# Branch hints on two long jumps, and three own-row gathers ahead of the branches, in a graph-attention and expert-mixture kernel

## The chip, the cores and the metric

The kernel runs on one core of a Trainium2 chip. The time is the device time of one execution in microseconds; the median of the runs is compared. The core has a matrix engine (PE, with its weight loads listed as PEld), a vector engine (DVE), an activation engine (ACT), a general engine (POOL) and a queue engine (SP). Each of them runs its own instruction stream, and all branch for themselves: a condition in the program is a register load and a compare-and-branch on every engine. They wait for each other through semaphores. An instruction that the engine's queue handles alone (a branch, a register load, a semaphore wait) is listed in the profile with a q behind the engine's name and is not counted as busy.

## The reference

1250 nodes with 512 features, 21,250 directed edges sorted by destination. A normalised graph-attention layer is added to `x`; its result is normalised again and goes into a mixture of four experts, each a two-layer SAGE convolution. Each node takes its two best experts.

```python
h = relu(layernorm(x));  x = x + attention(h, edges)
h = relu(layernorm(x))
gates = softmax(h @ gate_W + gate_b);  top_v, top_i = top_k(gates, 2)
for e in range(4):
    z = h
    for l in range(2):
        mean = segment_sum(z[src], dst) * inv_deg
        z = relu(mean @ Wl[e, l] + bl[e, l] + z @ Wr[e, l])
    expert[e] = z
out = x + sum(expert[top_i[n, k]][n] * top_v[n, k] for k in (0, 1))
```

## The kernel before, in words

`tile_sorted_graph` does everything for a graph whose edges are sorted; `tile_any_graph` is a second kernel behind it, which runs only if a count of the edges (`total`) does not come out as expected. Here it comes out, so the last branch, L1404, jumps over all of `tile_any_graph`.

The attention layer and the first aggregation take the first 220 us or so. Then the nodes that chose an expert are numbered (`number_slots`): per expert, its nodes fill places of 128 slots. `many[:, 0]` holds the number of nodes of each expert, `many[:, 1]` whether the number of places is odd; both are loaded into registers of all five engines where they are compared (`loaded`, L762).

The loop over experts starts at L1016. Layer 1 of an expert is computed for all 1250 nodes in five steps (`layer1`); its result goes to DRAM (`h1`) by SP and stays on chip in split form (`hs`). One step of the next expert's layer 1 is put behind the last one, to fill gaps. Layer 2 is computed only for the slots of the expert, place by place:

- The counts of edges of a place's nodes are gathered from DRAM by POOL (`fetch_counts`, L802), transposed and unpacked into a matrix (`unpack`); PE multiplies it with `hs` (`sums_of`, L935), which gives the neighbours' sums.
- The place's own rows of `h1` are gathered by POOL (`fetch_own`, L821) into a tile of the ring `hsels`, which has two tiles, and PE transposes them (`features`, L829).
- If the number of places is odd, `one_of_slots` does the first one alone, under the branch at L1041. The others are done two at a time by `pair_of_slots`, in five bodies nested in each other under the branches at L1043: where `counts[e] > i * 128` fails, the engine jumps over all the bodies that are left.
- A place's result is scattered into the output with addition, by POOL (`put`, L947).

Before the branch at L1041, two places' own rows are gathered (L1029). The third is gathered inside the first pair's body, as its first operation (L1048), and later pairs gather two places for the next pair after the transposes of their own. A new gather into a ring tile waits until the tile's last content has landed and been read.

Every engine runs its instructions in the order in which they were put; POOL's order of gathers, scatters and branches is therefore the order of the code. At the end of each expert POOL drains (L1067).

Of the kernel before, what the change touches and what calls it, by code (L numbers as in the profile page):

```python
# [9 lines left out]
F32 = mybir.dt.float32  # L10
# [3 lines left out]
I32 = mybir.dt.int32  # L14
U32 = mybir.dt.uint32
AF = mybir.ActivationFunctionType
OP = mybir.AluOpType
AX = mybir.AxisListType

SLOPE = 0.2  # L20
EPS = 1e-5
# [21 lines left out]
def tile_sorted_graph(  # L43
# [27 lines left out]
    nc = tc.nc  # L71
    N, D = x.shape
    E = src.shape[0]
    NE = gate_W.shape[1]
    T = 125
    NT = N // T
# [20 lines left out]
    const = ctx.enter_context(tc.tile_pool(name="const", bufs=1))  # L97
# [37 lines left out]
    SLOTS = 128  # L135
    NS = -(-N // SLOTS) + 1
# [15 lines left out]
    nc.gpsimd.memset(many_edges, float(1 << 15))  # L152
    ones_h = const.tile([128, 128], BF16, name="ones_h")
    nc.vector.memset(ones_h, 1.0)
    many = const.tile([1, 2, NE], I32, name="many")
    AT = adj.tile([T, NT, N], F32R, name="AT")
    AT32 = AT.bitcast(F32)

# [114 lines left out]
    for name in ("dst", "src"):  # L273
# [5 lines left out]
        i = build.tile([EB, NB], F32, name=f"i_{name}")  # L279
# [7 lines left out]
    for k in range(KF):  # L287
        for half in range(2):
# [3 lines left out]
                                           op0=OP.mult, op1=OP.mult,  # L292
# [14 lines left out]
    for half in range(2):  # L307
# [3 lines left out]
                                       op0=OP.mult, op1=OP.mult, accum_out=bw_b[:, half, HD:])  # L311
# [352 lines left out]
    def number_slots():  # L664

        flat = chosen.rearrange("p e t -> p (e t)")
        p = bank("p_n")
        nc.tensor.matmul(p[:T, :NE * NT], before, flat, start=True, stop=True)  # L670
        nc.tensor.matmul(p[:T, NE * NT:2 * NE * NT], ones_h[:T, :T], flat, start=True, stop=True)
        pv = p[:T, :2 * NE * NT].rearrange("p (a e t) -> p a e t", a=2, e=NE)
        off = book.tile([T, NE, NT + 1], F32, name="off")
        nc.vector.memset(off[:, :, 0], 0.0)
        for t in range(NT):
            nc.vector.tensor_add(off[:, :, t + 1], off[:, :, t], pv[:, 1, :, t])
        nc.vector.tensor_copy(many[:, 0, :], off[:1, :, NT])

        odd = book.tile([T, NE], F32, name="odd")
        twos = book.tile([T, NE], F32, name="twos")  # L680
        nc.vector.tensor_scalar(odd, off[:, :, NT], 1.0 / SLOTS, 0.5 - 0.25 / SLOTS, op0=OP.mult,
                                op1=OP.add)
        nc.vector.tensor_scalar(odd, odd, ROUND, -ROUND, op0=OP.add, op1=OP.add)
        nc.vector.tensor_scalar(twos, odd, 0.5, -0.25, op0=OP.mult, op1=OP.add)
        nc.vector.tensor_scalar(twos, twos, ROUND, -ROUND, op0=OP.add, op1=OP.add)
        nc.vector.scalar_tensor_tensor(odd, twos, -2.0, odd, op0=OP.mult, op1=OP.add)
        nc.vector.tensor_copy(many[:, 1, :], odd[:1, :])
        at = book.tile([T, NE, NT], F32, name="at")
        nc.vector.tensor_add(at, pv[:, 0], off[:, :, :NT])
        at = at.rearrange("p e t -> p (e t)")  # L690
        qt = book.tile([T, NE * NT], F32, name="qt")
        nc.vector.tensor_scalar(qt, at, 1.0 / SLOTS, -(0.5 - 0.25 / SLOTS), op0=OP.mult, op1=OP.add)
        nc.vector.tensor_scalar(qt, qt, ROUND, -ROUND, op0=OP.add, op1=OP.add)
        nc.vector.scalar_tensor_tensor(at, qt, float(-SLOTS), at, op0=OP.mult, op1=OP.add)

        by_expert = qt.rearrange("p (e t) -> p e t", e=NE)
        nc.vector.tensor_tensor(by_expert, by_expert, odd[:, :, None].to_broadcast([T, NE, NT]),
                                op=OP.subtract)
        nc.vector.scalar_tensor_tensor(qt, qt, 2.0, flat, op0=OP.add, op1=OP.mult)
        left = book.tile([T, NE, NT], F32, name="left")  # L700
        nc.vector.tensor_copy(left, g.rearrange("p t e -> p e t"))
        left = left.rearrange("p e t -> p (e t)")
        for f in range(2, FLD):
            nc.vector.tensor_copy(told[:, :, f], left)
            if f + 1 < FLD:
                nc.vector.tensor_sub(left, left, told[:, :, f])
        for e in range(NE):
            c = slice(e * NT, (e + 1) * NT)
            nc.vector.tensor_tensor(spots[:, c, :], steps_h[:, None, :].to_broadcast([T, NT, SLOTS]),
                                    at[:, c, None].to_broadcast([T, NT, SLOTS]), op=OP.is_equal)  # L710

        mine = mix_tiles[0][0].rearrange("p k n -> p (k n)").bitcast(BF16)[:T, :NE * NT * NS].rearrange(
            "p (c q) -> p c q", q=NS)
        nc.vector.tensor_tensor(mine, steps_h[:, None, 1:NS + 1].to_broadcast([T, NE * NT, NS]),
                                qt[:, :, None].to_broadcast([T, NE * NT, NS]), op=OP.is_equal)
        nc.vector.tensor_tensor(tells, mine[:, :, None, :].to_broadcast([T, NE * NT, FLD, NS]),
                                told[:, :, :, None].to_broadcast([T, NE * NT, FLD, NS]), op=OP.mult)
# [41 lines left out]
    nc.tensor.matmul(p[:T, :1], ones[:T, :T], sums[:, :1], start=True, stop=True)  # L759
    nc.vector.tensor_copy(total, p[:1, :1])  # L760

    def loaded(v, most):  # L762
        return nc.values_load(v, min_val=0, max_val=most,
                              skip_runtime_bounds_check_because="it is compared, and addresses nothing")

    counts, odds = ([loaded(many[:1, i, e:e + 1], N) for e in range(NE)] for i in range(2))
# [23 lines left out]
    packeds = Ring(1, [T, SLOTS], I32, "packed")  # L790
    digs = Ring(2, [T, 2, SLOTS], I32, "digs")
    ASs = Ring(2, [T, NT, SLOTS], F32R, "AS")
    hsels = Ring(2, [SLOTS, D], F32, "hsel")
    rTs = Ring(2, [128, KF, SLOTS], F32, "rT")
    gTs = Ring(2, [128, KF, SLOTS], F32, "gT")
    aggs = Ring(1, [SLOTS, D], F32, "agg")
# [22 lines left out]
    def fetch_own(j, h1):  # L819
        r = hsels()  # L820
        nc.gpsimd.indirect_dma_start(r, None, h1, bass.IndirectOffsetOnAxis(reads[:, j:j + 1], 0))  # L821
        return r
# [193 lines left out]
    for e in range(NE):  # L1016
        now.loads()
        for t in range(min(e, 1), NT // 2):
            now.layer1(t)
            if e == 0 and t == NT // 2 - 2:  # L1020
                asel = [fetch_counts(e * NS + i) for i in range(4)]
            if t == NT // 2 - (1 if e == 0 else 2):
                AS = [unpack(asel.pop(0)) for _ in range(2)]
                if e + 1 == NE:
                    third = wts[(e + 1) % 2].tile([128, KF, D], F32R, name="wl0")
                    third = third.rearrange("p k n -> p (k n)")[:T, :NT * SLOTS]
                    AS.append(unpack(asel.pop(0), third.rearrange("p (s n) -> p s n", s=NT)))
        now.finish()
        own = [fetch_own(e * NS + i, now.h1) for i in range(2)]  # L1029
        of = now  # L1030
        if e + 1 < NE:
            now = Expert(e + 1)
            now.layer1(0)
        mixing = of.mix_second()
        second = next(mixing)
        of.spare_sums = node_sums[4:] + \
            [vs.tiles[(vs.n + i) % 4] for i in range(2)]
        hs, h1 = of.hs, of.h1
        A, iv = AS.pop(0)
        r = own.pop(0)  # L1040
        with tc.If(odds[e] > 0):  # L1041
            one_of_slots(second, r, sums_of(A, hs), iv, e, 0)
        with ExitStack() as nest:  # L1043
            for i in range(1, NS, 2):
                nest.enter_context(tc.If(counts[e] > i * SLOTS))
                j = e * NS + i
                if i == 1:
                    own.append(fetch_own(j + 1, h1))  # L1048
                    if len(AS) < 2:
                        AS.append(unpack(asel.pop(0)))  # L1050
                    second = next(mixing)
                    asel.append(fetch_counts(j + 3))
                p = [sums_of(a, hs) for a, _ in AS]
                ivs = [iv for _, iv in AS]
                g = [mean_of(p[0], ivs[0])]
                r = [features(v, rTs, AF.Relu) for v in own]
                if i + 2 < NS:
                    own = [fetch_own(j + 2 + n, h1) for n in range(2)]
                    AS = [unpack(asel.pop(0)) for _ in range(2)]
                g.append(mean_of(p[1], ivs[1]))  # L1060

                asel += [fetch_counts(j + n) for n in range(4, 6) if i + n < NS]
                pair_of_slots(second, r, g, of.spare_sums, e, i)
        if e + 1 < NE:
            asel = [fetch_counts((e + 1) * NS + i) for i in range(4)]

        tc.keep_in_program_order(nc.gpsimd.drain())  # L1067
# [329 lines left out]
@with_exitstack  # L1397
def tile_gat_then_moe_sage(ctx: ExitStack, tc: tile.TileContext, *args):
    nc = tc.nc
    flag = ctx.enter_context(tc.tile_pool(name="flag", bufs=1))  # L1400
    total = flag.tile([1, 1], I32, name="total")
    counted = tile_sorted_graph(tc, *args, total)
    E = args[1].shape[0]
    with tc.If(counted != E):  # L1404
        tile_any_graph(tc, *args)


# [26 lines left out]
```

## Time and profile before

| what | value |
|---|---|
| median of 3 runs | 770.07 us (769.75 to 770.88) |
| the profiled execution | 766.87 us |
| its span, first to last instruction | 765.1 us |
| mean granted clock of PE | 0.985 |
| places of slots that ran (scatters of L947) | 22 |
| own gathers (L821) / gathers of counts (L802) | 31 / 35 |
| L1043 branches of each engine | 17 |
| transfers of code: queue q8, queue q14 | 35 packets of 0.57 MB, 36 of 0.29 MB |

The profile is one execution. A line of a timeline gives the start in us from the span's start, the busy time, the engine, the line of the code, the operation, the tiles (written <- read) and how often it stands there; in square brackets is how long the engine had stood idle before it, and what released it. A line of waits gives the engine and its operation, behind the arrow what it waited for, and then the total in us, how often, and the longest. A line of queue instructions gives how many, their shortest, median and longest duration in ns, and the starts of the first and the last in us. A window's line gives, for PE, PEld, DVE, ACT and POOL, the busy time and in brackets the number of instructions, then PE's granted clock (1.00 is full), the DMA engines' busy share and GB/s.

### The profile page before, as it was taken

The numbers are of one execution on the slowest core, as the hardware profiler recorded it, in microseconds if no ns is written. First come the engines' busy times: TensorE is split into PE (matmuls) and PEld (weight loads), VectorE is DVE, ScalarE is ACT, GpSimd is POOL, SyncE is SP. The second block draws the span as 40 slices with busy tenths as digits, with TensorE's granted clock in tenths as the row PEclk, the third lists the DMA queues.
The fourth block names the chain that finished last, engine by engine and source line by source line (L and its number), as shares of the span: only waits on it lengthen the run. The fifth ranks groups of instructions, "written<-read, shape, count | busy, mean of one in ns | idle before, by whom it ended". The sixth has DMA issues, their size and how long they took to land. (4 is left out here: it accounts for less than half of the span.)

```text
span 765.1 us, 9962 instructions
## 1 busy us (share of the span) xinstructions
PE 718.2 (94%) x3413; PEld 581.3 (76%) x3413; DVE 515.3 (67%) x1345; ACT 247.6 (32%) x569; POOL 160.4 (21%) x140
## 2 busy tenths in 40 slices
PE   6799989898999999889999999999999999999893
PEld 4677444445999888778878888888888888888782
DVE  7987999799888559336965544568464554657542
ACT  4559656865300112110313332103031333104320
POOL 1001425222002001120033332300142331400441
PEclk9899999999999999989999999999999999999997
DMA  7000001010135412181223133631132322601332
GB/s 199 5 7 5 3 7 58 8 41 1 48 131 175 127 41 70 29 280 39 68 76 58 43 56 56 193 126 41 43 80 44 59 46 45 181 28 56 79 62 31
DMA packets 30147, 52.46 MB, mean 69 GB/s; under 512 B 7132, under 2 KB 8326, under 8 KB 30076
## 3 DMA queue, kind: packets, MB, share of 16 engines
q0 software_dynamic: 6768, 15.51, 11.0%
q1 hardware_dynamic: 15154, 20.18, 8.8%
q10 hardware_dynamic: 8154, 15.91, 6.0%
q8 instruction: 35, 0.57, 0.3%
q14 instruction: 36, 0.29, 0.1%
HBM read 33.03 MB, written 19.20 MB: 68 GB/s over the span
## 5 line engine op out<-in xcount | busy, mean ns | idle before, releaser
L429 PE MATMUL p_o<-hW,P 125*125 125x512 f32 x200 | 91.8, 599 | 3.8 <-DVE P L423 3.7
L935 PE MATMUL p_s<-h_hi,AS 125*128 125x512 f32 x210 | 83.9, 399 | 0.9 <-DVE v L907 0.9
L115 ACT ACTIVATE h_hi<-v 125x512 fp32r<-125x512 f32 x40 | 24.9, 629 | 181.4 <-DVE v L904 144.7
L935 PE MATMUL p_s<-h_lo,AS 125*128 125x512 f32 x210 | 82.0, 390 | 0.0
L839 PE MATMUL p<-T,S 128*125 128x256 f32 x320 | 73.4, 381 | 0.4 <-DVE v L888 0.2
L839 PEld LDWEIGHTS p<-T,S 128*125 128x125 f32 x320 | 60.2, 189 | 10.6 <-DVE v L888 1.6
L941 DVE TENSOR_SCALAR agg<-p_s,asel 128x512 f32<-128x512 f32 x22 | 16.5, 750 | 76.4 <-PE p_f L829 39.4
L816 ACT CAST AS<-digs 125x256 fp32r<-125x256 int32 x150 | 54.8, 403 | 36.9 <-DVE digs L340 31.2
L821 POOL DMA_INDIRECT hsel<-h,reads x31 | 36.1, 1164 | 141.9 <-issue 51.0
L429 PEld LDWEIGHTS p_o<-hW,P 125*125 125x125 f32 x200 | 35.3, 188 | 39.4 <-issue 32.6
L947 POOL DMA_INDIRECT out_dram<-y,writes x22 | 35.8, 1626 | 118.1 <-ACT y L983 47.8
L427 POOL TENSOR_TENSOR den<-den,P 125x375 f32<-125x375 f32 (+1 forms) x27 | 39.3, 1454 | 57.9 <-DVE P L423 51.8
L340 DVE TENSOR_SCALAR digs<-packed 125x128 int32<-125x128 int32 x279 | 45.7, 221 | 3.0 <-ACT packed L810 2.2
L802 POOL DMA_INDIRECT asel<-packs,reads x35 | 38.4, 1097 | 39.3 <-DVE agg L941 25.1
L935 PEld LDWEIGHTS p_s<-h_hi,AS 125*128 125x128 f32 x210 | 39.5, 188 | 9.4 <-issue 1.3
L831 ACT ACTIVATE gT<-p_f 128x512 f32<-128x512 f32 x22 | 13.6, 616 | 99.9 <-PE p_f L829 99.9
L935 PEld LDWEIGHTS p_s<-h_lo,AS 125*128 125x128 f32 x210 | 39.5, 188 | 8.1
L839 PE MATMUL p<-wr,h2T 128*125 128x256 f32 x160 | 39.9, 394 | 6.0 <-DVEq L1043 4.9
L327 PE MATMUL p_h<-W_sb,hT 128*125 128x257 f32 x160 | 40.7, 412 | 3.1 <-ACT hT L184 3.0
L554 PE MATMUL p_ag<-AT,h_hi 125*128 125x416 f32 (+1 forms) x120 | 42.4, 355 | 0.0
L554 PE MATMUL p_ag<-AT,h_lo 125*128 125x416 f32 (+1 forms) x120 | 42.1, 353 | 0.0
L381 DVE TENSOR_SCALAR first<-iota,low,val 125x125 bf16<-125x125 f16 x128 | 40.8, 384 | 0.0
(238 smaller groups left out, 1461.3 us busy)
## 6 DMA issues: line engine op xcount, KB each, us to landing
h<-v SPq DMA_DIRECT2D x40, 224.0 KB
wl<-in_L_gnn_Wl_dram ACTq DMA_DIRECT2D x7, 1024.0 KB
wr<-in_L_gnn_Wr_dram ACTq DMA_DIRECT2D x7, 1024.0 KB
out_dram<-x SPq DMA_DIRECT2D x10, 224.0 KB
x<-in_x_dram SPq DMA_DIRECT2D x1, 1120.0 KB
h<-v SPq DMA_DIRECT2D x40, 26.0 KB
W_sb<-in_L_gnn_W_dram SPq DMA_DIRECT2D x4, 256.0 KB
wl<-in_L_gnn_Wl_dram SPq DMA_DIRECT2D x1, 1024.0 KB
```

The source lines that it names most:

```text
L327: nc.tensor.matmul(p[:T, :HD + 1], hT[:, k, :], W_sb[:, k, half, :], start=(k == 0), stop=(k == KF - 1))
L340: nc.vector.tensor_scalar(o, v, BITS * d, (1 << BITS) - 1, op0=OP.logical_shift_right, op1=OP.bitwise_and)
L381: nc.vector.tensor_scalar(hs[:, :T], iota[:EB, :T], low[:, j:j + 1], val[:, j:j + 1], op0=OP.is_equal, op1=OP.mult)
L427: nc.gpsimd.tensor_add(den[:, :n], den[:, :n], P[:, :n])
L429: nc.tensor.matmul(po[i][:T, :], P[:, i * T:(i + 1) * T], hW[:, s - 1, :, :HD], start=(s == 1), stop=(s == NT))
L554: nc.tensor.matmul(p[:, :n], h2[s][i][:, m * 128:(m + 1) * 128], AT[:, s, c], start=(s == 0 and i == 0), stop=(s == NT - 1 and i == 1))
L802: nc.gpsimd.indirect_dma_start(a, None, packs, bass.IndirectOffsetOnAxis(reads[:, j:j + 1], 0))
L816: nc.scalar.copy(AS[:, d:d + 2, :], dig)
L821: nc.gpsimd.indirect_dma_start(r, None, h1, bass.IndirectOffsetOnAxis(reads[:, j:j + 1], 0))
L839: nc.tensor.matmul(p, A[:, k, :], B[:, k, :], start=(i == 0 and k == 0), stop=(i * KF + k == n - 1))
L935: nc.tensor.matmul(p, A[:, s, :], hs[s][f], start=(s == order[0] and f == 0), stop=(s == order[-1] and f == 1))
L947: s = nc.gpsimd.indirect_dma_start(out, bass.IndirectOffsetOnAxis(writes[:, j:j + 1], 0), y, None, bounds_check=N - 1, oob_is_err=False, c ...
```

## The change

Three things are edited.

1. The two kinds of jump get a name (`label`), and a hint instruction is put ahead of the branch. For the first pairs branch of expert 0 (`pairs0`) it stands ahead of the branch at L1041, on DVE and POOL only, and takes its value from a register: a new row of `many`, 1 if the expert has more than 128 nodes (the body runs) and 0 if not (the jump is taken). For the branch around `tile_any_graph` (`general`) it stands in the first pair body of the last expert, on PE, DVE, ACT and POOL, with no register: the jump is expected to be taken.
2. The third gather of own rows moves from the first pair's body to the two others, ahead of both branches of the expert, in every expert.
3. The ring `hsels` gets a third tile.

`loaded` now names the engines; its default is the same five as before.

```diff
+ET = mybir.EngineType
+HINTED = [ET.PE, ET.DVE, ET.Activation, ET.Pool]
...
-    many = const.tile([1, 2, NE], I32, name="many")
+    many = const.tile([1, 3, NE], I32, name="many")
...
         nc.vector.tensor_copy(many[:, 1, :], odd[:1, :])
+        nc.vector.tensor_scalar(many[:, 2, :], off[:1, :, NT], SLOTS + 0.5, None, op0=OP.is_gt)
...
-    def loaded(v, most):
-        return nc.values_load(v, min_val=0, max_val=most,
+    def loaded(v, most, engines=(*HINTED, ET.SP)):
+        return nc.values_load(v, engines=engines, min_val=0, max_val=most,
...
-    hsels = Ring(2, [SLOTS, D], F32, "hsel")
+    hsels = Ring(3, [SLOTS, D], F32, "hsel")
...
-        own = [fetch_own(e * NS + i, now.h1) for i in range(2)]
+        own = [fetch_own(e * NS + i, now.h1) for i in range(3)]
...
         hs, h1 = of.hs, of.h1
+        if e == 0:
+            some = (ET.DVE, ET.Pool)
+            tc.mark_branch_hint_location("pairs0", hint=loaded(many[:1, 2, :1], 1, some), engines=some)
         A, iv = AS.pop(0)
         r = own.pop(0)
         with tc.If(odds[e] > 0):
             one_of_slots(second, r, sums_of(A, hs), iv, e, 0)
         with ExitStack() as nest:
             for i in range(1, NS, 2):
-                nest.enter_context(tc.If(counts[e] > i * SLOTS))
                 j = e * NS + i
+                nest.enter_context(tc.If(counts[e] > i * SLOTS, label="pairs0" if j == 1 else None))
+                if e + 1 == NE and i == 1:
+                    tc.mark_branch_hint_location("general", engines=HINTED)
                 if i == 1:
-                    own.append(fetch_own(j + 1, h1))
                     if len(AS) < 2:
                         AS.append(unpack(asel.pop(0)))
...
-    with tc.If(counted != E):
+    with tc.If(counted != E, label="general"):
         tile_any_graph(tc, *args)
```

## The prediction

> **What bounds the kernel now.** I read the page's engine table first, then who waited for whom on PE, then the one gap that this list names in PE's own timeline, then the tail behind the last transfer.
>
> ```profile
> span 765.1 us, 9962 instructions
> PE 718.2 (94%) x3413; PEld 581.3 (76%) x3413; DVE 515.3 (67%) x1345; ACT 247.6 (32%) x569; POOL 160.4 (21%) x140
> ```
>
> PE is busy 94% of the span. From 200 to 300 us the list of waits has no entry for PE, so work added there on DVE (busier than PE in places) costs nothing. From 300 us on, PE waited for this (releaser; us in total, times, longest):
>
> ```profile
> PE p L839 <- DVEq L1043: 4.9, 1, 4.9
> PE p_f L829 <- DMA hsel<-h,reads: 2.4, 1, 2.4
> PE p L839 <- DVE y L991: 1.1, 2, 0.5
> PE p_s L935 <- DVE v L907: 0.9, 1, 0.9
> ```
>
> Two gaps matter. The first is released by DVE's queue at L1043, the nested branch, and not by an operation. PE's timeline around it, and DVE's queue there (start of first and last):
>
> ```profile
> 321.62 1.89 PE L839 MATMUL p<-T,agT 128*125 128x256 f32 x8
> 328.45 3.75 PE L839 MATMUL p<-wr,h2T 128*125 128x256 f32 x8 [4.95 <-DVEq L1043]
> ```
> ```profile
> L1043 DVEq COMPARE_BRANCH  x1: 69/69/69, 324.0 to 324.0; - x1
> L1043 DVEq EVENT_SEMAPHORE  x1: 21/21/21, 328.3 to 328.3; - x1
> ```
>
> Expert 0 has one place of slots (the L947 rows are 1, 8, 9 and 4 for the four experts), so its first nested branch jumps over five pair bodies. DVE branches at 324.0 for 0.07 and runs its next instruction at 328.3: 4.2 us of nothing, in which the trace has an 8 KB transfer of the instruction queue q14 (326.4). PE's own branch shows the same as a long duration, with a 16 KB transfer of q8 inside it (322.2, 1.1 us):
>
> ```profile
> L1043 PEldq COMPARE_BRANCH  x1: 3512/3512/3512, 321.2 to 321.2; - x1
> L1043 PEldq EVENT_SEMAPHORE  x1: 51/51/51, 324.8 to 324.8; - x1
> ```
>
> So PE is ready at 324.8 and stands until 328.45 for DVE alone. The gap costs more than itself. Windows by stage (after the sums and engine columns: granted clock, DMA share, GB/s):
>
> ```profile
> 323.00:328.00 5.00, 0.51 (x3) 0.10 (x1) 0.42 (x1) 0.00 (x0) 0.18 (x1) 0.77 0.54 126
> 328.00:330.00 2.00, 1.54 (x4) 1.29 (x5) 0.00 (x0) 0.00 (x0) 0.89 (x1) 0.50 0.42 42
> ```
>
> The clock went to 0.50 at 325.7 and back to 1.00 at 332.5; the eight matmuls at 328.45 took 3.75 us, where eight of that shape take 1.89 before.
>
> The second gap is in expert 3, whose first pair has nothing of a next expert beside it:
>
> ```profile
> 712.90 0.94 POOL L821 DMA_INDIRECT hsel<-h,reads  x1 [2.28 <-PE p_f L829]
> 716.31 0.66 PE L829 MATMUL p_f<-ident,hsel 128*128 128x128 f32 x4 [2.45 <-DMA hsel<-h,reads]
> ```
>
> The gather issued last holds PE for 2.45. Last, the tail: POOL's last scatter starts at 754.0 and lands at 759.1; then POOL's queue reaches the branch around the general kernel, L1404, and again jumps:
>
> ```profile
> L1404 POOLq COMPARE_BRANCH  x1: 55/55/55, 760.2 to 760.2; - x1
> L1404 POOLq EVENT_SEMAPHORE  x1: 17/17/17, 762.8 to 762.8; - x1
> ```
>
> 2.5 us stand between them. PE passes L1404 at 758.1, DVE at 758.4, SP at 706.0; so POOL alone sets the end of 765.1.
>
> **The change part by part.**
>
> *Hint on the first pairs branch, DVE and POOL.* No row of before shows a hint, so bounds first. At worst it does nothing; at best DVE resumes as after its other taken branches, 0.05 to 0.5 us behind them (L1043 at 485.5: 0.3). Then DVE is through at 324.0 + 0.07 + 0.3 = 324.4. What is late next is PE's own jump, which gets no hint here: 324.8, plus its semaphore and first weights, 0.15 as at 328.3 to 328.45, so 325.0. Saved: 328.45 - 325.0 = 3.45. PE then stands 1.5 us. The gap of 2.45 in expert 3 kept a clock of 1.00, so I expect no slow stretch: the first ten matmuls after 328.45 spread over 4.2 us where 0.216 each makes 2.15, saved 2.05. Together 5.5. Behind it PE has no wait over 0.6 until 702, and the weight loads that ACT issues after waiting for DVE (328.4) move ahead with it, so the gain is kept. I take the full value, because the hint stands 17 us ahead of the branch (DVE's previous branch is at 306.5) and the fetch itself took under 4.3. Its price: one register load on DVE (L763 DVEq rows, 0.30 to 0.91), inside the 4.42 us that DVE stands before L941 at 311.25; on POOL (0.28 to 0.51) inside 16 us idle before 321.1. If that cover were gone, at most 1 us. POOL needs no such hint: it went on 0.13 after its branch at 321.4. The new comparison in number_slots is one 4-element DVE operation (L681: 0.15) at about 220, where PE waits for nothing.
>
> *Third gather ahead of the branches, ring of three.* In expert 3 the gathers start at 707.64, 709.68 and 712.90. The third waits until 712.2, when the first has landed, because with two tiles it overwrites that one; it also stands behind two branches of POOL. With three tiles it follows the second after 0.94 and the usual 0.30, at 710.9, and lands 3.41 later as before (712.90 to 716.31): 714.3. PE is free at 713.87, so it waits 0.5 in place of 2.45: 2.0 saved, and behind it every row of expert 3 shifts. Queued behind the moved gather on POOL are the register load, the scatter of an odd place and the gathers of counts; in expert 2 it moves from 560.2 to about 542.7 with POOL idle until 558.1, in expert 1 from 389.7 to 387.9, and PE waits for none of these. Expert 0 gets one gather more (about 305.3, 0.94 us, its rows unread), with POOL idle behind it. The free third tile also ends much of POOL's 41.0 us of waiting for p_f; PE does not wait for those, so nothing.
>
> *Hint on the general branch, four engines.* It is put into expert 3's first pair body, four instructions; no row has their cost, nearest are POOL's register moves and branches, 0.03 to 0.07, on PE inside its 0.95 wait at 702. PE, DVE and ACT are off the path at the end. For POOL the 2.5 goes to between 0.13 (its taken L1043 at 753.8, next instruction at 754.0) and 0.38 (SP at L1404); I take 0.2: 2.3 saved. Late next are SP's waits, done at 760.4, the same instant, then POOL's drain of 1.36 and the closing handshake as now.
>
> Sum: 5.5 + 2.0 + 2.3 = 9.8. The profiled execution took 766.87 around its span of 765.1; it would become 757.1. The median of the runs is 770.07, 3.2 above it; I take the same difference off the median: **760.3**.
>
> **A rule against the change.** The trace shows that each long jump ends with a transfer on an instruction queue. The Trainium skill (Runtime: NRT & Kernel Launch, Instruction fetch mechanics) says that prefetch of code is purely sequential, and that a taken branch to a page outside the current two forces a fetch before execution goes on; it knows no hint. By it both hints do nothing and the change is worth 2.0. The trace of before agrees with its second half (4.2, 3.5 and 2.5 us) and cannot show the first.
>
> **The rivals.**
>
> 1. *Hints do not act* (0.13). Only the gather's 2.0 is left: 768.1. For it: no row shows a hint acting. Against it: a branch 17 us away leaves time.
>
> 2. *The first hint comes too late, the last one acts* (0.15). The q14 transfers near DVE are at 294.3, 321.7 and 326.4, and DVE has 64 recorded rows from 294 to its branch. If the one at 294.3 already filled DVE's next block, a hint at 306 finds the slot taken. Then 2.0 + 2.3 are left: 765.8.
>
> 3. *The first acts, POOL's last does not* (0.08), since POOL lands only 6 us ahead of L1404: 5.5 + 2.0, so 762.6.
>
> 4. *Slower* (0.12). A hint takes the slot of the next block at once and holds it until its branch. The last hint is armed at about 705, and four engines then run 45 us of straight code. PE fetches at 729.9 and 749.9 in this stretch, DVE crosses about one border. DVE's would cost what L1043 costs today, 4.95 + 2.05 = 7.0; PE's two each 3.5 less the 2.3 that its queue ran ahead at 321.2, up to 5.6 without that lead and with the slow clock: 9.4 to 18.2 against 9.8 saved, so -0.4 to +8.4, in the middle +4: 774. It decides once PE's two crossings cost over 1.4 each. Against it: PE's queue passes its branch at 725.7 while the matmuls ahead of it run until 729.7, a lead of 4.
>
> **How the numbers follow.** The forecast has 0.52. Cases to 768.1 hold 0.88 with it; the low end adds 1.8 below 760.3 for a jump of PE that shortens too (its 1.5 left) and rounding, the high end is rival 1 and 0.5: 758.5 to 768.6. A measurement tells about 0.2%, 1.5 us, from no change: forecast and rivals 2 and 3 are faster (0.75), rival 1 at 2.0 is mostly so (0.08, and 0.05 within), rival 4 is slower (0.12).
>
> **What would show it.** Right: DVE's first instruction behind its L1043 within 0.5 us; PE's gap there about 1.5, with a clock of 1.00 until the end; a q14 transfer between 306 and 323; expert 3's three gathers 1.2 apart, PE's wait there under 0.7; POOL's L1404 pair under 0.4 apart. Wrong: DVE still 4 us late at L1043 (rivals 1, 2); new long branch or idle "issue" rows on PE and DVE in expert 3 (rival 4); a clock of 0.50 after a gap of 1.5.

## The result and the profile after

The changed kernel takes **760.29 us** (median of 4 runs, 759.65 to 761.53); the kernel before, timed beside it, takes 770.48 (769.75 to 772.25). The ratio is 0.9866 with an interval of 0.9845 to 0.9888. In a later comparison (`after_again`, below) it was 762.07 against 769.58, ratio 0.9893 [0.9864, 0.9922]. So the change gains 1.1 to 1.3%, and the forecast of 760.3 holds. Its terms do not all hold, and that is what the rest is about.

The profiled execution of the changed kernel took 760.18 us. Line numbers have moved: the nested branch is L1049 (was L1043), the last branch L1411 (L1404), the own gathers L824 (L821), the scatter L950 (L947). First the page's first lines, then what PE waited for from 300 us on:

```profile
span 758.5 us, 9991 instructions
PE 717.9 (95%) x3413; PEld 580.6 (77%) x3413; DVE 516.4 (68%) x1346; ACT 247.7 (33%) x569; POOL 158.9 (21%) x141
```
```profile
PE p L842 <- DVEq L1049: 2.3, 1, 2.3
...
PE p_f L832 <- DMA hsel<-h,reads: 0.4, 1, 0.4
```

PE's work is the same; its two named waits went from 4.9 to 2.3 and from 2.4 to 0.4. PE's timeline around the first one, the queue instructions there, and the window with PE's granted clock:

```profile
323.87 1.89 PE L842 MATMUL p<-T,agT 128*125 128x256 f32 x8
328.05 1.96 PE L842 MATMUL p<-wr,h2T 128*125 128x256 f32 x8 [2.29 <-DVEq L1049]
```
```profile
L1049 PEldq COMPARE_BRANCH  x1: 3974/3974/3974, 323.6 to 323.6; - x1
L1049 DVEq COMPARE_BRANCH  x1: 79/79/79, 327.3 to 327.3; - x1
L1049 PEldq EVENT_SEMAPHORE  x1: 51/51/51, 327.6 to 327.6; - x1
...
L1049 DVEq EVENT_SEMAPHORE  x1: 21/21/21, 327.9 to 327.9; - x1
```
```profile
328.00:330.00 2.00, 1.95 (x9) 1.75 (x10) 0.00 (x0) 0.00 (x0) 0.00 (x0) 1.00 0.62 145
```

DVE's 4.2 us of nothing behind its branch is gone: the next instruction follows 0.54 later. PE's own branch, which got no hint, still takes 4.0. The clock stays at 1.00, and the eight matmuls take 1.96 where they took 3.75. But PE stands 2.29 and not 1.5, for two reasons. PE's own branch took 3.97 instead of 3.51 and lands 1.89 into the gap, where before's landed 1.30 into it; with the 0.15 behind a landing that the prediction took, that alone makes a gap of about 2.05. And DVE comes to its branch only at 327.3, 0.3 before PE lands, so DVE is through last and adds the other 0.2. Behind the second reason is a row that I had not expected, DVE's load of the count in front of that branch (first the changed kernel's, then before's):

```profile
L766 DVEq TENSOR_LOAD <-many x1: 1368/1368/1368, 325.8 to 325.8; - x1
```
```profile
L763 DVEq TENSOR_LOAD <-many x1: 316/316/316, 323.6 to 323.6; - x1
```

Then expert 3's gathers (POOL), with PE's wait for the third, and POOL's queue at the last branch:

```profile
704.20 1.88 POOL L824 DMA_INDIRECT hsel<-h,reads  x1 [38.08 <-SPq L1411]
706.38 0.95 POOL L824 DMA_INDIRECT hsel<-h,reads  x1 [0.30 <-DVE wr L928]
707.63 0.95 POOL L824 DMA_INDIRECT hsel<-h,reads  x1 [0.30 <-issue]
```
```profile
711.41 0.66 PE L832 MATMUL p_f<-ident,hsel 128*128 128x128 f32 x4 [0.44 <-DMA hsel<-h,reads]
```
```profile
L1411 POOLq COMPARE_BRANCH  x1: 68/68/68, 755.6 to 755.6; - x1
L1411 POOLq EVENT_SEMAPHORE  x1: 17/17/17, 756.1 to 756.1; - x1
```

The third gather is issued 1.25 behind the second instead of 3.22, and POOL's 2.5 at the last branch became 0.5. One new entry stands earlier, in the list of PE's waits from 200 to 300 us, which was empty before; beside it DVE's queue there has the load that the first hint needs:

```profile
PE p L842 <- DVE v L891: 0.6, 1, 0.6
```
```profile
L766 DVEq TENSOR_LOAD <-many x1: 548/548/548, 241.6 to 241.6; - x1
```

The load and the hint stand on DVE at 241.6 and 242.3, ahead of an addition that PE waits for, and not at 306 where I had placed them; POOL's hint stands at 222.9. So an engine's order need not be the order of the source, POOL's neither.

**Where the time went.** PE runs the same 3413 matmuls in the same order in every kernel here, so I subtract the start of one matmul in before's profiled execution from its start in another kernel's: negative is earlier. The step at the pairs branch is the change of this difference between matmuls 1400 and 1500 (319 to 348 us in before), that of expert 3 between matmuls 3200 and 3300 (706 to 730), that at 242 us between 900 and 1100. "Until 36 us" is the difference at matmul 100; the tail is what lies behind the last matmul. "Slow clock" is the length of the stretch with a granted clock of 0.5 that begins in PE's gap at the pairs branch or right behind it; before has 6.8.

| kernel | until 36 us | at 242 us | pairs branch | slow clock there | expert 3 | tail |
|---|---|---|---|---|---|---|
| changed kernel | +1.44 | +0.88 | -4.65 | none | -2.71 | -1.82 |
| after_again | +1.96 | +0.36 | -2.86 | 3.4 | -2.38 | -1.25 |
| gather_only | +0.02 | 0.00 | +0.08 | 6.8 | -2.96 | +0.43 |
| ring3_only | +1.87 | 0.00 | +0.15 | 6.8 | -0.64 | -0.16 |
| pairs0_only | -0.03 | +0.36 | -4.60 | none | +0.78 | -0.31 |
| pairs0_inverted | +1.02 | +0.36 | -0.10 | 6.8 | -3.19 | -2.13 |
| general_only | +0.95 | 0.00 | +0.07 | 6.8 | +2.53 | -2.43 |
| in_odd_body | +0.52 | +0.23 | -2.91 | 3.4 | -3.14 | -1.49 |
| in_odd_body_pe | +0.55 | +0.15 | -2.78 | 3.4 | -1.60 | -2.07 |
| dve_only | +1.04 | +0.89 | -4.57 | none | -1.67 | -1.77 |
| dve_pe_odd | +2.93 | +0.21 | -2.62 | 3.4 | -3.12 | -1.97 |
| late_scatter | +2.25 | +0.22 | -5.30 | none | -3.08 | -1.71 |
| before_again | +1.64 | 0.00 | +0.35 | 6.8 | +0.08 | -0.27 |

Each row is one execution. The first column has nothing to do with the change: the kernel before itself (`before_again`) shows +1.64 there. The column of expert 3 holds waits and, where a slow stretch follows them, its cost. The times, from many executions:

| kernel | median, lowest to highest (runs) | before beside it | ratio and interval |
|---|---|---|---|
| gather_only | 764.98, 764.02 to 767.76 (7) | 770.70 | 0.9941 [0.9920, 0.9962] |
| pairs0_only | 763.84, 762.87 to 764.63 (5) | 770.70 | 0.9919 [0.9896, 0.9942] |
| general_only | 765.02, 763.61 to 770.05 (12) | 770.70 | 0.9946 [0.9926, 0.9966] |
| pairs0_inverted | 763.20, 761.59 to 763.97 (5) | 770.70 | 0.9906 [0.9882, 0.9930] |
| ring3_only | 766.27, 763.16 to 768.23 (11) | 769.71 | 0.9952 [0.9930, 0.9975] |
| in_odd_body | 761.65, 760.05 to 764.87 (6) | 769.71 | 0.9906 [0.9878, 0.9934] |
| in_odd_body_pe | 761.08, 760.03 to 764.12 (5) | 769.71 | 0.9899 [0.9869, 0.9930] |
| dve_only | 760.99, 757.65 to 762.64 (6) | 769.58 | 0.9885 [0.9855, 0.9915] |
| dve_pe_odd | 761.94, 758.46 to 764.32 (6) | 769.58 | 0.9899 [0.9868, 0.9930] |
| after_again | 762.07, 758.48 to 763.10 (6) | 769.58 | 0.9893 [0.9864, 0.9922] |
| late_scatter | 758.32, 756.91 to 759.26 (5) | 767.37 | 0.9871 [0.9847, 0.9895] |

### The profile page after: what moved, and what is told of

The parts are those of the page before. It is cut to its first block, busy times and chain, and to the rows that moved or that the text cites. A ratio compares the mean times of both kernels' runs of the same rounds, so it can differ in the third digit from the quotient of the medians.

```text
span 758.5 us, 9991 instructions
## 1 busy us (share of the span) xinstructions
PE 717.9 (95%) x3413; PEld 580.6 (77%) x3413; DVE 516.4 (68%) x1346; ACT 247.7 (33%) x569; POOL 158.9 (21%) x141
## 5 line engine op out<-in xcount | busy, mean ns | idle before, releaser
L824 POOL DMA_INDIRECT hsel<-h,reads x32 | 35.9, 1122 | 132.4 <-issue 42.7
L950 POOL DMA_INDIRECT out_dram<-y,writes x22 | 35.4, 1607 | 131.0 <-ACT y L986 59.1
L805 POOL DMA_INDIRECT asel<-packs,reads x35 | 36.3, 1038 | 33.5 <-DVE agg L944 19.7
L842 PE MATMUL p<-wr,h2T 128*125 128x256 f32 x160 | 38.1, 381 | 3.4 <-DVEq L1049 2.3
L329 PEld LDWEIGHTS p_h<-W_sb,hT 128*125 128x125 f32 x160 | 32.8, 210 | 10.7 <-ACT hT L186 5.0
```

The source lines that it names most:

```text
L329: nc.tensor.matmul(p[:T, :HD + 1], hT[:, k, :], W_sb[:, k, half, :], start=(k == 0), stop=(k == KF - 1))
L805: nc.gpsimd.indirect_dma_start(a, None, packs, bass.IndirectOffsetOnAxis(reads[:, j:j + 1], 0))
L842: nc.tensor.matmul(p, A[:, k, :], B[:, k, :], start=(i == 0 and k == 0), stop=(i * KF + k == n - 1))
L950: s = nc.gpsimd.indirect_dma_start(out, bass.IndirectOffsetOnAxis(writes[:, j:j + 1], 0), y, None, bounds_check=N - 1, oob_is_err=False, c ...
```

## The experiments

The theory after the result: three separate gains, namely the hinted jump on DVE, the third gather, and POOL's last jump, less a price of the hint's load at 242 us. Rivals: the gains come from moved code and not from the hints; an armed hint makes later code stall; the gather gains by its new place and not by its tile.

### One part alone: gather_only, pairs0_only, general_only

gather_only has the third tile and the moved gather and no hint; pairs0_only has the first hint (with the new row of `many`); general_only has the last hint.

> Only the third gather moved ahead of the branches and the ring of three; no hint. Theory (each part acts by itself, as the two traces read): PE's wait for hsel in expert 3 falls from 2.45 us to about 0.4, and PE's rows behind it come 2.0 to 2.8 us earlier; the gap at L1043 stays at about 5 us and POOL's at the last branch at 2.5; so 2 to 3 us faster than before. Rival (the gain of expert 3 comes from the hints, by moved code or by POOL's earlier register load): the wait stays at about 2.4 and the time does not change.

> Only the hint on the first pairs branch, on DVE and POOL, with its comparison and register load; gather and ring as before, no hint on the last branch. Theory: DVE goes on within 0.6 us behind its jump, PE's gap falls from 4.95 to 2.3 us with the clock at 1.00 behind it, worth 4.4 to 4.7; the register load that the hint brings to DVE at about 241 us delays PE by 0.9; net 3.5 to 3.9 us faster. The wait in expert 3 stays at 2.4 and POOL's last gap at 2.5. Rival (code merely moved to other places in its blocks, so that the landing was there by luck): PE's gap is back at 5 us in this other layout.

> Only the static hint on the branch around the general kernel, on four engines, in the last expert's first pair body. Theory: POOL's gap behind that branch falls from 2.5 us to 0.5 and the end comes 1.7 to 2.1 us earlier; everything ahead is as before, 5 us gap and all. Rival (a hint that stays armed for 45 us takes the place of the next block): long stalls on PE or DVE between 705 and 755 us, and no gain.

Each part is faster alone, by 0.6, 0.8 and 0.5%. The rows show each gain at its own place in the table: -2.96 in expert 3, -4.60 at the pairs branch, -2.43 in the tail. The times of the two single hints hold one thing more. Where the third gather still makes PE wait, the wait can drop PE's clock. PE's timeline and the windows of general_only (the last three columns are clock, DMA share, GB/s):

```profile
717.88 0.66 PE L831 MATMUL p_f<-ident,hsel 128*128 128x128 f32 x4 [2.78 <-DMA hsel<-h,reads]
```
```profile
716.00:719.00 3.00, 1.12 (x8) 0.93 (x9) 0.00 (x0) 0.37 (x1) 2.39 (x3) 1.00 0.49 118
719.00:723.00 4.00, 4.00 (x15) 3.26 (x14) 2.57 (x11) 2.41 (x7) 2.85 (x3) 0.57 0.55 140
```

The +2.53 of the table is 0.5 of longer waits (this one and one of 0.81 just ahead) and 2.0 behind them, nearly all of it from the slow stretch of 3.4 us whose clock is the 0.57 of the second window. pairs0_only has such a stretch from 711.3 to 714.7, behind a wait of 2.13: some 1.8 lost to it, less 1.1 of shorter waits, make its +0.78. Before's profiled execution had a wait of 2.45 and kept its clock. So gather_only gains 3.0 against an execution that keeps its clock, and would gain 5.5 against one like general_only's (2.96 + 2.53); I had given the part 2.0. In general_only there is no new wait between 705 and 755: an armed hint does not make the straight code behind it stall, and the slower rival (4) falls.

### The hint with the wrong value: pairs0_inverted

```diff
-        nc.vector.tensor_scalar(many[:, 2, :], off[:1, :, NT], SLOTS + 0.5, None, op0=OP.is_gt)
+        nc.vector.tensor_scalar(many[:, 2, :], off[:1, :, NT], SLOTS + 0.5, None, op0=OP.is_le)
```

All the changed kernel's instructions are there, at the same places; the hint now names the way that is not taken.

> The whole change, with one comparison turned round (less or equal in place of greater), so that the register of the first hint says that the jump is not taken. The same instructions in the same places; only the hint's value is wrong. Theory (the fetch that the hint starts is what helps): DVE stalls about 4.2 us behind its jump again, PE's gap is 5 us with the slow clock behind it, and the time is 4.4 to 5 us above the changed kernel's, about 765. Rival (the layout or the early register loads help): gap of 2.3 as in the changed kernel, the same time.

DVE's queue at the branch:

```profile
L1049 DVEq COMPARE_BRANCH  x1: 69/69/69, 325.3 to 325.3; - x1
...
L1049 DVEq EVENT_SEMAPHORE  x1: 21/21/21, 329.3 to 329.3; - x1
```

The 3.9 us are back, PE waits 4.62 and the slow clock follows. The step at the pairs branch is -0.10 where the changed kernel has -4.65. The time was 763.20, lower than the 765 expected; the executions differ in their first 36 us, and the ratio's interval just reaches that of the changed kernel. Against `after_again`, whose step is -2.86, the difference of the steps is 2.8, about that of the medians (2.9). The rows decide: the value in the hint's register makes the difference, and not where code lies. The Trainium skill (Runtime: NRT & Kernel Launch, Instruction fetch mechanics) says that prefetch of code is purely sequential. The hinted kernels' 0.54 against 3.9 here speak against that sentence; its next one, that a taken branch out of the window waits for a fetch, agrees with the 3.9.

### The tile without the move: ring3_only

```diff
-    hsels = Ring(2, [SLOTS, D], F32, "hsel")
+    hsels = Ring(3, [SLOTS, D], F32, "hsel")
```

> The ring of three alone: the third gather stays in the first pair's body, behind both branches. Theory (the third gather was late because it overwrote the first one's tile and waited for its landing, and not because of its place): in expert 3 the third gather follows the second after about 1.25 us, PE waits 0.3 to 0.5 us for hsel in place of 2.1 to 2.8, and the time is that of the gather and ring together, 765 within 1. Rival (its place behind POOL's two branches matters): the third gather still starts 2 us or more behind the second, and less than half of the gain comes.

The third gather, still behind two branches on POOL, starts 1.26 after the second (709.41, 710.68, 711.94). So the tile freed it, and its place did not matter. PE's list of waits in this kernel:

```profile
PE p_y L839 <- DVE digs L340: 2.0, 1, 2.0
...
PE p_f L829 <- DMA hsel<-h,reads: 0.3, 1, 0.3
```

The old wait is 0.3, but in this execution a new one of 2.0 stood right behind it, so expert 3 gained 0.64 only. ACT was late twice by some 2 us there (its copies of `rT` and `gT` at 718.1 and 720.9). Why is open. The move alone, with two tiles, wasn't tried: the gather would overwrite a tile that is still to be read.

### Another place, one engine more: in_odd_body, in_odd_body_pe

The hint at 242 us costs 0.36 to 0.89 in the five executions that have it there. Inside the odd body it stands at 308 us, where the load has cover:

```diff
         with tc.If(odds[e] > 0):
+            if e == 0:
+                some = (ET.DVE, ET.Pool)
+                tc.mark_branch_hint_location("pairs0", hint=loaded(many[:1, 2, :1], 1, some), engines=some)
             one_of_slots(second, r, sums_of(A, hs), iv, e, 0)
```

In in_odd_body_pe `some` is `(ET.PE, ET.DVE, ET.Pool)`.

> The whole change, but the first hint (DVE and POOL) and its register load stand at the start of expert 0's odd body, at about 309 us, so that they cannot be put at 242 us. Theory (15 us ahead of the branch is lead enough, and the load at 242 cost PE 0.3 to 0.9): DVE goes on within 0.6 us behind its jump, PE's gap there stays 2.3, the 0.6 us wait on L891 at 243 goes, and the time is 0.3 to 0.9 below the changed kernel's 760.3. Rival (DVE has been in the branch's block since about 296 and has its next block already, so that a hint at 309 finds the slot taken): DVE stalls 4 us again, PE's gap is 5 with a slow clock, 764 to 765.

> As the run before this one, with PE hinted on the first pairs branch too. Theory (PE's own fetch is what is left of the gap, and its transfer beside DVE's register load makes that load slow, 1.37 us in place of 0.32): PE's branch takes under 0.5 us in place of 3.4 to 4.0, DVE's load of the count falls to 0.3 to 0.5, PE's gap falls from 2.3 to about 1.2, and the time is 1 us below the run without PE. Rival (DVE is late by itself, behind the last vector operation and its load): the gap stays at 2 or more although PE's branch is short.

The price at 242 falls to 0.15 to 0.23 (the rest is not explained), DVE again resumes 0.60 behind its branch, so a lead of 18 us is enough and rival 2 falls. Neither is faster than the changed kernel. In in_odd_body_pe PE's branch and then the matmuls behind the gap:

```profile
L1049 PEldq COMPARE_BRANCH  x1: 381/381/381, 322.3 to 322.3; - x1
```
```profile
326.70 3.57 PE L842 MATMUL p<-wr,h2T 128*125 128x256 f32 x8 [2.54 <-DVEq L1049]
```

PE's jump falls from 3.4 to 0.38 and PE stands as long as before, 2.54, for DVE, whose load takes 1.56. So with PE's jump gone the bound is that load. And both executions have a slow clock of 3.4 us behind the gap, which with the slightly longer gap takes some 1.8 off the step (-2.9 and -2.8 instead of -4.65). That is no matter of the place: the unchanged copy `after_again` has it too.

### Why DVE's load takes 1.4: dve_only, dve_pe_odd, after_again

In the executions so far with the first hint at its right value the load took 1.37 to 1.63 us, in all others 0.32 to 0.33. My first theory was POOL's hint. dve_only is the changed kernel with `some = (ET.DVE,)`, dve_pe_odd is in_odd_body_pe with `(ET.PE, ET.DVE)`, after_again is the changed kernel.

> The changed kernel with the first hint on DVE alone, in its place ahead of the odd branch. Theory (POOL's scatter in front of the load): load 0.3 to 0.4 us instead of 1.37, DVE's gap behind L1049 0.5 to 0.6, and PE's gap 1.2 to 2.0 instead of 2.29, since PE's own jump of 3.5 to 4.0 us now ends last there: 759.3 to 760.3 against the changed kernel's, at most 1.0 below it. Rival (armed hint slows the load): load 1.4 to 1.6, gap 2.3, the same time as the changed kernel within 0.5.

> The first hint stands at the start of expert 0's odd body as in in_odd_body_pe, on PE and DVE, and POOL is left out. Theory: POOL's hint is what makes DVE slow. In all four runs with POOL hinted DVE's load of the count took 1.37 to 1.63 us, in the six others 0.31 to 0.33; in the former POOL issues its scatter (L950) directly behind the branch's join, and the load falls into that scatter's traffic. So here DVE's load is back at 0.3 to 0.4 us, PE's gap behind its pairs branch falls from 2.3 to 2.6 to 1.0 to 1.4, no slow clock follows it, and the time is 758.5 to 760.0, 1 to 2.5 below in_odd_body_pe's 761.08; POOL's own jump takes 2.0 to 2.5 us again and costs nothing, its next operation being the gathers of the second pair. Rival (DVE's load is slow because DVE's own hint is armed, whatever POOL does): the load stays at 1.4 to 1.6, PE's gap at 2.3 to 2.6, the time at 760.5 to 761.5.

> The changed kernel unedited, for the comparison on one chip: 759.6 to 761.5 and a ratio of 0.985 to 0.989; DVE's load of the count 1.4 to 1.6 us, DVE's gap behind L1049 0.5 to 0.6, PE's gap 2.3 to 2.6. If a slow clock falls into PE's gap as in in_odd_body, it is a matter of the single execution and not of the place of the hint; then the groups of times lie 1.5 to 2.5 apart.

The theory fell: without POOL's hint the load takes 1.44 and 1.64, PE waits 2.37 and 2.63. after_again came out as expected but for its time, 0.6 above the range: its gap of 2.39 has the slow clock (-2.86), which the first profile's 2.29 had not.

Sorting the 13 executions by the load's duration shows what goes with it. First before's rows (POOL's scatter; DVE's operation at the same time), then the changed kernel's:

```profile
321.12 2.06 POOL L947 DMA_INDIRECT out_dram<-y,writes  x1 [16.15 <-ACTq L1043]
```
```profile
321.00 0.68 DVE L643 TENSOR_TENSOR S<-h2T 128x500 f32<-128x500 f32 x1
```
```profile
323.36 1.63 POOL L950 DMA_INDIRECT out_dram<-y,writes  x1 [14.36 <-ACT y L1014]
```
```profile
323.38 0.70 DVE L645 TENSOR_TENSOR S<-h2T 128x500 f32<-128x500 f32 x1
```

In the six executions with the short load, the scatter starts 0.12 us inside this DVE operation, takes 2.06, and its transfers on queue 0 start 2.8 to 2.9 behind its start. In the seven with the long load, it starts 0.01 to 0.27 ahead of the operation, takes 1.63, and its transfers start at 2.2. DVE's load stands 2.44 to 2.45 behind the scatter's start in all 13. So it comes just before the transfers in the first group, and into them in the second. What moved the DVE operation, by 0.13 to 0.39, is the hint itself: DVE's branch out of the odd block takes 0.080 to 0.086 with it at its right value and 0.047 to 0.051 in the others (pairs0_inverted among them), and the operations behind it follow later; why is open. Before has a witness for the price too, SP's load, most of it beside the transfers:

```profile
L763 SPq TENSOR_LOAD <-many x1: 922/922/922, 323.8 to 323.8; - x1
```

One thing more differs between the groups: queue 1, by the times of SP's issues its rows of `h1`, starts a burst of transfers 0.38 to 0.40 ahead of the six short loads, and from 0.14 ahead of the seven long ones to 0.08 behind their start. The Trainium skill (GPSIMD Engine Reference, Specifications) says that GpSimd shares its way to on-chip memory with the vector engine, and that operations of that engine with two inputs there contend with it. The operation above is such a one, a difference of two parts of `h2T`. That the scatter's time changes with its place against this operation (2.06 or 1.63) fits; but the two overlap in both groups, and the rule does not say why the scatter is the faster one where it starts first. That is open.

### The scatter made later: late_scatter

dve_pe_odd, with a second relu in expert 0 (it changes no value and takes ACT 0.63 us):

```diff
         nc.scalar.activation(y, y, AF.Relu, scale=gate[:, e, i:i + 1])
+        if e == 0:
+            nc.scalar.activation(y, y, AF.Relu)
         put(y, e, i)
```

> dve_pe_odd, and the first place's scatter (L950) made about 0.7 us later: ACT applies its relu of L1014 twice in expert 0 (0.72 us each; the second changes no value). Theory, formed after dve_only and dve_pe_odd refuted that POOL's hint is the cause: a hint on DVE makes DVE leave the odd block 0.13 us later (branch 86 ns instead of 51); POOL's scatter then starts just ahead of DVE's 0.67 us operation of L645 instead of 0.12 us inside it, takes 1.63 instead of 2.06, and its transfers on queue 0 start 2.2 instead of 2.9 us behind its start; DVE's load of the count, always 2.445 us behind that start, falls into them and takes 1.37 to 1.64 instead of 0.31 to 0.33. With the scatter 0.7 later the transfers start behind the load: load 0.3 to 0.4 us, PE's gap behind its pairs branch 1.2 to 1.5 instead of 2.6, no slow clock behind it, 1.1 to 2.5 of time below dve_pe_odd's 761.94, so 759.4 to 760.8. Rival (the load is slow because DVE's hint is armed, whatever POOL's scatter does): load still 1.4 to 1.6, gap 2.4 to 2.6, time as dve_pe_odd, 761 to 762.5.

POOL's scatter, DVE's load, and PE's first matmuls behind the gap:

```profile
324.19 1.78 POOL L950 DMA_INDIRECT out_dram<-y,writes  x1 [15.48 <-ACT y L1016]
```
```profile
L766 DVEq TENSOR_LOAD <-many x1: 647/647/647, 326.0 to 326.0; - x1
```
```profile
327.55 1.96 PE L842 MATMUL p<-wr,h2T 128*125 128x256 f32 x8 [1.63 <-DVEq L1051]
```

Nothing of the hint was touched, the load fell from 1.64 to 0.65, PE's gap from 2.63 to 1.63, and no slow clock follows: the step at the pairs branch is -5.30, the largest seen. The armed hint does not slow the load by itself; the place of the scatter against it does, and the times of its transfers fit in all 14 executions. It did not reach 0.3: queue 0 starts 0.2 behind the load's end here, but queue 1's burst starts within 0.01 of the load's start, as near as in the seven long ones. So the last 0.3 is probably queue 1's: DVE's loads of before at 559.7 and 703.3, with no transfer of a scatter beside them but over 100 of queue 1, took 0.62 and 0.91. No run takes queue 1 away. The time of 758.32 is the lowest of all and below the 759.4 expected. But before was lower in that comparison as well (767.37), and the ratio of 0.9871 cannot be told from the changed kernel's 0.9866. So it beats before; its rows show a shorter gap than the changed kernel's, but that it is faster as a whole is not shown.

### before_again

The kernel before once more, one execution with a profile.

> The kernel of before once more, for a second profile. 24 runs of it lie in two groups, 766.2 to 768.3 and 769.5 to 771.9, and the first profiled execution (766.87) is of the lower one. Theory (in the upper group the second gap, PE's wait for hsel in expert 3, is followed by a slow stretch of the clock, as it was in two of the experiments): if this run is of the upper group, its clock goes to 0.50 at 711 to 720 us and the rows behind come 2.5 to 4 us later; if it is of the lower group there is none. Rival (the difference lies at the start, where the first slow stretch is 6.8 us in some runs and 10.2 in others): the rows are late from 30 us on and nothing happens in expert 3.

It took 768.71, 1.84 above the first profile. Most of it stands in the first 36 us (+1.64), where the first slow stretch of the clock lasts 10.2 us instead of 6.8, as the expectation's rival had it; a further stretch at 174 us cost nothing, and PE's two waits are 5.0 and 2.5 as before.

## Why the prediction was right

The forecast was right, and all three gains came by the mechanisms that it named. Their sizes were off on both sides, and three smaller steps failed: the place of the hint's load, the clock behind a gap, and the median's distance from the profile.

- *DVE's jump goes.* Right: 0.54 behind the branch (forecast within 0.5), the slow clock gone in the profile. pairs0_inverted shows that the hint's value did it. The step measured 4.65 of the 5.5, and 2.86 in `after_again`.
- *"What is late next is PE's own jump", gap 1.5.* Wrong in part. PE's jump does land late (327.6), but DVE, 0.3 ahead of it at its branch, is still released last. Two terms were mis-sized. PE's jump was taken at before's 3.51, landing 1.30 into the gap; in the five executions with DVE hinted and PE not, it took 3.4 to 4.0 and landed 1.4 to 1.9 into it, so it alone makes 1.5 to 2.05. DVE's load in front of the branch, 0.32, became 1.37 to 1.63, since the hint moves DVE against POOL's scatter; that adds 0.2 in the changed kernel's profile and 0.4 to 0.9 in the other four. With PE hinted too (in_odd_body_pe) the gap did not shrink; with the load shortened (late_scatter) it came to 1.63.
- *A gap of this length keeps the clock at 1.00.* Only sometimes. Of seven executions with gaps of 2.3 to 2.6, four show a slow stretch of 3.4 us, and their steps are 2.6 to 2.9 instead of 4.6. The four are the longest, 2.39 to 2.63 against 2.29 to 2.37; but length alone does not decide, since in expert 3 a wait of 2.13 lost the clock and one of 2.45 kept it. I had taken one wait of 2.45 in one execution as a rule. At 1.63 it held, in one execution.
- *The hint's load costs nothing at 306 us.* Wrong: it stood at 241.6 on DVE, ahead of an addition that PE waits for, and cost 0.36 to 0.89. I had read the place from the source, and DVE's order in the trace is another. The forecast's "at most 1 us if that cover were gone" covers it.
- *Third gather, 2.0.* Right in mechanism, and the tile alone does it (ring3_only). Size: 2.7 in the profile, 1.6 to 3.2 in those of the kernels with the moved gather. The rest is a second wait for a gather just ahead (0.65 at 713.2 in before, which the view put down to ACT; before_again lists it under the gather, 3.0 in two waits). Against an execution whose clock drops in the wait it is worth up to 5.5.
- *POOL's last jump, 2.3.* Right: 2.5 became 0.48, so 2.0; the forecast was 0.2 for the rest. The other hinted engines lose only a part of their stall there (DVE 3.7 to 2.1, ACT 2.5 to 1.2, PE's branch 3.7 to 1.8), off the path; why is open.
- *A q14 transfer between 306 and 323.* Not found: the changed kernel has none between 297 and 323. No view says which engine a transfer of queue 14 is for, so which of those at 296.3, 324.0 and 325.0 brought DVE's code is open.
- *The median lies 3.2 above the profile.* This step failed. I carried it over as a constant; after the change the median is 0.1 above its own profile (760.18). Before's first profile was a lucky one: it had the short slow stretch at the start (1.6 less than `before_again`) and, as `before_again` did, kept its clock in expert 3. The changed kernel's sum is 6.6 from span to span (765.1 to 758.5), not 9.8. Of the 3.2 between them 1.44 is that start, 0.88 the load at 242, 0.85 the pairs branch, 0.5 the tail and 0.25 lies between the branch and expert 3, less 0.7 that the gather gave more. Median to median it is 10.2 and, in the later comparison, 7.5, since the median of before also pays for drops of the clock: its executions of 766 to 767.5 have a mean granted clock of 0.985 or 0.986, those of 770 and more 0.975 to 0.981. That the sum and the median meet at 760.3 is partly luck.

Rival 1 falls with pairs0_inverted, rival 2 with in_odd_body, rival 3 with POOL's 0.48, rival 4 with general_only.

## What to carry to other kernels

Where a long jump holds an engine for 2.5 to 4.3 us and the way is known 18 us ahead or more, a hint can take most of it away, though at the last branch it left DVE, ACT and PE about half; check where its register load lands in the engine's order, not in the source. When a stall is removed, look at every instruction between the last unchanged one and the branch, since a shift of 0.1 to 0.4 us can put a load into a burst of transfers. And do not carry one profile's distance to the median: find which stretches of slow clock the profile has, and count them as terms with a chance.

## What the runs showed that I had not expected

- A hint instruction takes 0.04 to 0.07 us. At the pairs branch DVE resumes 0.5 to 0.6 us behind the long jump and PE's branch takes 0.38, against 3.9 to 4.3 and 3.4 to 4.0 without it. At the last branch POOL resumes after 0.5 instead of 2.5 to 2.8, but DVE after 1.9 to 2.5, ACT after 1.2 to 1.5, and PE's branch takes 1.0 to 1.8 (3.0 to 3.7, 2.5 to 2.6 and 3.7 to 4.3 without it).
- A register load from on-chip memory took 0.27 to 0.33 us at its fastest, up to 0.91 beside queue 1's transfers and no scatter's (though 0.32 in the six short ones above, with 61 to 65 of them under way), and 0.5 to 1.6 beside a scatter's.
- PE's slow clock comes in stretches of 3.4, 6.8 or 10.2 us, and a gap of 2.1 to 2.8 us can set one off or not, in different executions of one kernel too (2.29 and 2.39 in the changed kernel); a stretch of 3.4 behind such a gap cost 1.4 to 2.0 us.
- Expert 0's scatter (POOL) took 1.63 us when it started just ahead of a two-input DVE operation of 0.68, 2.06 when it started 0.12 inside it, and 1.78 when 0.40 inside it.
